# Three loads behind a scatter in a new order, and one block's transposes moved by a few matmuls

## The chip, the cores and the metric

The kernel runs on one core of one Trainium2 chip. The metric is the device time of one execution in microseconds; the figures are medians over several executions. One further execution was taken with the hardware profiler, and every duration below is from that one.

## What is computed

One layer over 4096 tokens of 256 features: a dense graph layer, then causal attention with rotary embeddings, then a mixture of 8 experts of which each token takes two.

```python
x = x + gnn(layernorm(x), adj)            # x: (4096, 256), adj: (4096, 4096)
x = x + ffn(layernorm(x))

def gnn(f, adj):
    h = adj @ (f @ neigh_W.T) / (adj.sum(axis=1, keepdims=True) + 1.0)
    return concatenate([f, h], axis=-1) @ lin_W.T

def ffn(x):                               # one sequence of 4096 tokens
    h = rmsnorm(x)
    q, k, v = ...                         # 4 heads, 2 key/value heads of 64, rotary
    y = softmax(causal(q @ k.T / 8)) @ v
    x = x + y @ wo.T
    flat = rmsnorm(x)
    probs = softmax(flat @ router_w.T)
    ...                                   # the two largest of 8, made to sum to one
    out = sum over e of weight[:, e] * ((silu(flat @ w1[e].T) * (flat @ w3[e].T)) @ w2[e].T)
    return x + out
```

All data are float32. The experts have 682 hidden features.

## The kernel before

The order of the instructions on each engine is the order in which the program writes them (`tc.manual_schedule()`, L94). Semaphore waits between engines follow from the tiles that are read and written. SyncE (SP) issues nearly all loads, GpSimd (POOL) the scatters. An instruction that waits holds back everything behind it on its own engine.

**The graph layer (L253 to L682).** Tokens lie in eight blocks of 512. `adj` comes as 64 blocks of 512 x 512 (1 MB each) through three buffers (`load(n)`, L268). `aggregate(b, steps)` (L510) makes the products of one row of eight adjacency blocks with the normalised features `g[jb]`. Each block's 2 x 2 product of sub-blocks is made with seven products instead of eight, from sums that VectorE (DVE) makes: `halve(n)` (L478) the sums S1 to S4 of an adjacency block, `halve_x(b)` (L455) the sums T1 to T4 of the features. The first products of a block (A11, A12) take the adjacency block as it was loaded. After the fourth product (`i == 3`, L538) `aggregate` calls the list `steps[jb]`, and after the seventh `steps[jb, "end"]`. The preparation of later feature blocks stands in these lists:

- `scales_x(b)` (L437): mean and variance on VectorE, the inverse deviation on GpSimd
- `normed_x(b, t)` (L443): VectorE writes the normalised block into `g[b]`. It is called from `features(b - 1)`
- `turned_x(b)` (L450): eight transposes on TensorE (L431) into two banks, two copies by ScalarE (L433)
- `features(b)` (L494): `normed_x` of the block after it, then eight matmuls in the program (L503, sixteen in the trace), added to the residual by VectorE (L508)

Blocks 0, 1 and 2 are turned before `aggregate` starts, in the startup sequence L635 to L658; blocks 3 to 7 in the `"end"` lists.

**Attention (from L686)** goes over the blocks in a fixed order and keeps TensorE in matmuls of scores and values. At its end it also routes tokens: rows of normalised tokens, with their gates, are scattered in device memory (`lists`) by expert.

**The expert groups (L1875 to L1923).** The rows of each expert are cut into groups: 25 whole groups of 256 rows and, of 128 rows, up to 21 half groups. The loop runs over the first 42 of them (`NM`) in the order `TURNS`. For group `k`:

- `load_rows(k)` (L1393) loads the rows, 265 KB or half of it. The room is a ring of five; that of group k + 4 held group k - 1, whose scatter takes its row numbers from it. So this load waits until the scatter of group k - 1 has landed
- `load13(k)` (L1379) loads w1 and w3 of the group's expert (1408 KB), `load2(k)` (L1386) loads w2 (768 KB), both into rings of five. `load13` and `load_rows` first read their expert or place from a table
- `prepare(k)` (L1407) turns the rows on TensorE, during the group before
- `hidden(k)` (L1672) or, for 13 of the whole groups, `hidden_seven(k)` (L1486) makes the hidden features. The second form needs sums of w1 and w3, which GpSimd makes some groups ahead: `sums13` (L1451, L1463 to L1466)
- `combine(k)` (L1726) makes the products with w2, the gates are applied (L1765 or L1771), and GpSimd scatters each half with an added sum into `acc_dram` (L1776). A scatter waits until the group's before has landed

In iteration k, after `combine(k - 1)`, GpSimd writes a one-element tile and SyncE copies it out (`sent`, L1910 and L1911). As GpSimd takes instructions in order, SyncE passes this marker only once the scatter of group k - 1 has been issued. Then SyncE issues the loads for later groups: rows of k + 4, w2 of k + 4, w13 of k + 5. At k = 39 the accumulated rows are copied to the output (L1922); the last three groups are scattered into the output itself.

```python
            if 0 < k < NM - 1:
                combine(k - 1)
                if k + 4 < NM:
                    nc.gpsimd.memset(sent, 0.0)
                    nc.sync.dma_start(sent_dram, sent)
            if k + 4 < NM:
                load_rows(k + 4)
                load2(k + 4)
            if k + 5 < NM:
                load13(k + 5)
```

Of the kernel before, what the change touches and what calls it, by code (L numbers as in the profile page):

```python
# [54 lines left out]
NM = NG - RARE  # L55
# [11 lines left out]
def fast_kernel(  # L67
# [185 lines left out]
    with (  # L253
# [171 lines left out]
        def transposed(src, dst):  # L425

            for h in range(2):
                tr = p_tr.tile([P, 2, 2, P], F32, tag="tr", name="tr")
                for t in range(2):
                    for c in range(2):  # L430
                        nc.tensor.transpose(tr[:, c, t, :], src(2 * h + t, c), ident)  # L431
                cols = slice(h * 2 * P, (h + 1) * 2 * P)
                nc.scalar.copy(dst[:, :, cols], tr.rearrange("p c t i -> p c (t i)"))  # L433
# [16 lines left out]
        def turned_x(b):  # L450

            turned[b] = qT[b % 4]
            transposed(lambda t, c: g[b][:, t // 2 * 2 + c, t % 2, :], turned[b])

        def halve_x(b):  # L455

            nc.scalar.copy(
                g[b][:, 1:4:2, :, HC - 1], ones[:, 0:4].rearrange("p (k t) -> p k t", k=2)
            )
            part = [g[b][:, k] for k in range(7)]  # L460
            nc.vector.tensor_sub(part[T1], part[G12], part[G11])
            nc.vector.tensor_sub(part[T3], part[G22], part[G12])
            nc.vector.tensor_sub(part[T2], part[G22], part[T1])
            nc.vector.tensor_sub(part[T4], part[T2], part[G21])
# [29 lines left out]
        def features(b):  # L494
            fT = turned.pop(b)
            for t in range(TB if b + 1 < NB else 0):
                normed_x(b + 1, t)
            for h in range(2):
                pj = p_pj.tile([P, 2, C], F32, tag="pj", name=f"pf_{b}_{h}")
                for t in range(2):  # L500
                    for c in range(2):
                        at = (2 * h + t) * P
                        nc.tensor.matmul(  # L503
                            pj[:, t, :], fT[:, c, at : at + P], l1_sb[:, c, :],
                            start=(c == 0), stop=(c == 1),
                        )
                x1 = res[b][:, 2 * h : 2 * h + 2, :]
                nc.vector.tensor_add(x1, x1, pj)  # L508
# [144 lines left out]
        scales_x(2)  # L653
        halve(0)
        features(1)
        turned_x(2)
        halve_x(1)
        scales_x(3)  # L658
        steps = {jb: [] for jb in range(NB)}
        for jb in range(NB):  # L660
            for f, b in (
                (halve, jb + 1), (features, jb + 2), (halve_x, jb + 2), (scales_x, jb + 4),
            ):
                if b < NB or f is halve:
                    steps[jb].append(lambda f=f, b=b: f(b))
            if jb + 3 < NB:
                steps[jb, "end"] = [lambda b=jb + 3: turned_x(b)]
        steps[3].append(load_rest)
        for jb, f in ((5, scale_rest), (6, bounds), (6, turn_wo), (7, router_wo)):
            steps[jb].append(f)  # L670
        behind, at_end = [], []
        for b in range(NB):
            if b:

                steps = {0: behind, (0, "end"): at_end}
# [10 lines left out]
    with (  # L686
# [360 lines left out]
        def free(inst, group, reason):  # L1047
            tc.declare_no_dep(inst.ins, group=group, reason=reason)

        def join(inst, group):  # L1050
            tc.add_to_no_dep_group(group, inst.ins)
# [288 lines left out]
        def entry(t, most):  # L1340
            return nc.values_load(
                t, engines=[SP], min_val=0, max_val=most,
                skip_runtime_bounds_check_because="the lists are as long as the tokens are many",
            )
# [31 lines left out]
        def halves(i):  # L1376
            return HALF if i < NW else 1

        def load13(k):  # L1379
            i = TURNS[k]  # L1380
            expert_of[i] = entry(table[0:1, 1, i : i + 1], NE - 1)
            nc.sync.dma_start(
                w13s[k % 5], w13[bass.ds(expert_of[i], 1)].rearrange("o p c w -> p (o c) w")
            )

        def load2(k):  # L1386
            i = TURNS[k]
            nc.sync.dma_start(
                w2s[k % 5],
                w2[bass.ds(expert_of.pop(i), 1)].rearrange("o p k c -> p (o k) c"),  # L1390
            )

        def load_rows(k):  # L1393
            i = TURNS[k]
            n = halves(i)
            at = entry(table[0:1, 0, i : i + 1], NE * REG - (GR if i < NW else 0))
            r = late[:, LATE_ROWS + k % 5 * 2 * ROW : LATE_ROWS + (k % 5 + 1) * 2 * ROW]
            r = r.rearrange("p (h c) -> p h c", h=HALF)
            get = nc.sync.dma_start(
                r[:, 0:n, :], lists[bass.ds(at, n * P), :].rearrange("(h p) c -> p h c", p=P)  # L1400
            )
            if i < NA:
                free(get, "late writes", "the rows of the first groups are whole by then")
                join(get, "first reads")
            rows[i] = r
# [45 lines left out]
        def sums13(k):  # L1451

            if not unsummed or unsummed[0] > k + 5 or len(sums13_of) == 2:
                return
            k = unsummed.pop(0)
            chunks = w13s[k % 5][:, :, 0 : 2 * NF * P].rearrange(
                "p c (k r i) -> p c r k i", r=2, i=P
            )
            m = {f"A{r + 1}{c + 1}": chunks[:, c, r] for r in range(2) for c in range(2)}
            for n, name in enumerate(("S1", "S2", "S4")):  # L1460
                m[name] = rooms13[SPLIT13.index(k) % 2][:, n]
            m["S3"] = m["A21"]
            nc.gpsimd.tensor_add(m["S1"], m["A21"], m["A22"])  # L1463
            nc.gpsimd.tensor_sub(m["S2"], m["S1"], m["A11"])
            nc.gpsimd.tensor_sub(m["S4"], m["A12"], m["S2"])
            nc.gpsimd.tensor_sub(m["S3"], m["A11"], m["A21"])  # L1466
            sums13_of[k] = m
# [151 lines left out]
        def sums2(k):  # L1619

            if k in parts_of:
                return
            m = {}
            for c in range(2):
                weights = w2s[k % 5].rearrange("p (j c) o -> p c j o", c=2)[:, c]
                for h in range(2):
                    m[f"G{c + 1}{h + 1}"] = weights[:, :, h * P : (h + 1) * P]
            for n, s in enumerate(("T1", "T2", "T4")):
                m[s] = vv[SEVEN.index(k) % 2 * 3 + n][:, 0:3, :]
            m["T3"] = m["G12"]  # L1630
            nc.vector.tensor_sub(m["T1"], m["G12"], m["G11"])
            nc.vector.tensor_sub(m["T3"], m["G22"], m["G12"])
            nc.vector.tensor_sub(m["T2"], m["G22"], m["T1"])
            nc.vector.tensor_sub(m["T4"], m["T2"], m["G21"])
            parts_of[k] = m
# [242 lines left out]
        def step():  # L1878
            for f in next(rest, []):
                f()  # L1880
# [8 lines left out]
        for k in range(NM):  # L1889
            if k == 3:  # L1890
                sc_scope.close()
                p_h.append(ctx_h.enter_context(tc.tile_pool(name="e_h", bufs=6, space=PSUM)))
            if k == NM - 1:


                between = iter([lambda: None, lambda: combine(k - 1)])
            if k in SPLIT13:
                hidden_seven(k, step, k + 1)
            else:
                hidden(  # L1900
                    k, step if k < NM - 1 else lambda: next(between)(),
                    k + 1 if k + 1 < NM else None,
                )
            step()
            if k + 1 in SPLIT13 and TURNS[k] >= NW:
                sums2(k + 1)
# [3 lines that stand above are left out]
                    nc.gpsimd.memset(sent, 0.0)  # L1910
                    nc.sync.dma_start(sent_dram, sent)  # L1911
            if k + 4 < NM:
                load_rows(k + 4)
                load2(k + 4)
            if k + 5 < NM:
                load13(k + 5)
            if 0 < k < NM - 1:
                step()
                if k >= ALONE and TURNS[k - 1] < NW:
                    sums13(k)  # L1920
            if k == NM - LAST:
                nc.sync.dma_start(out, acc_dram[0:N, :])  # L1922
# [741 lines left out]
```

## Time and profile before

| | us |
|---|---|
| median of three runs | 1541.14 |
| lowest and highest run | 1536.98, 1544.27 |
| the profiled execution, as timed | 1537.88 |
| its span, first to last instruction | 1535.9 |
| graph layer, roughly | 0 to 500 |
| attention and routing, roughly | 500 to 1020 |
| expert groups, roughly | 1030 to 1527 |
| last scatters landing | to 1535.9 |

The profile speaks of the engines as PE (matmuls), PEld (loading of weights into TensorE), DVE, ACT (ScalarE), POOL and SP. A line of a group gives line, engine, operation, the tile written and the tiles read. In a timeline line, the first two numbers are start and duration in us, and the bracket at the end says how long the engine had stood idle and what released it. A line of waits gives total, number and longest. A line of stretches gives its length, then for each engine the busy time and the instructions in brackets, and at the end the granted clock of TensorE, the busy share of the DMA engines and GB/s. "SPq" lines are DMA issues of SyncE. Queue q1 carries the loads of SyncE, q0 the scatters of GpSimd.

### The profile page before, as it was taken

The numbers are of one execution on the slowest core, as the hardware profiler recorded it, in microseconds if no ns is written. First come the engines' busy times: TensorE is split into PE (matmuls) and PEld (weight loads), VectorE is DVE, ScalarE is ACT, GpSimd is POOL, SyncE is SP. The second block draws the span as 40 slices with busy tenths as digits, with TensorE's granted clock in tenths as the row PEclk, the third lists the DMA queues.
The fourth block names the chain that finished last, engine by engine and source line by source line (L and its number), as shares of the span: only waits on it lengthen the run. The fifth ranks groups of instructions, "written<-read, shape, count | busy, mean of one in ns | idle before, by whom it ended". The sixth has DMA issues, their size and how long they took to land. (4 is left out here: it accounts for less than half of the span.)

```text
span 1535.9 us, 28140 instructions
## 1 busy us (share of the span) xinstructions
PE 1519.8 (99%) x10925; PEld 1123.7 (73%) x10925; DVE 1056.2 (69%) x2182; ACT 555.7 (36%) x989; POOL 557.6 (36%) x641
## 2 busy tenths in 40 slices
PE   8999999999999999999999999999999999999997
PEld 7888888888888544444444444358899999999996
DVE  7754665755755677779879878884665777675862
ACT  2102021021021455655665655652123334333331
POOL 2102122121221331374554653442424446354542
PEclk9999999999999999999999999999999999999999
DMA  6334544544544000010011011047766777777765
GB/s 240 125 123 149 174 141 144 157 149 136 178 139 153 5 1 24 21 58 30 30 58 37 29 37 36 22 185 281 215 211 196 241 255 229 255 247 231 265 186 133
DMA packets 69594, 212.15 MB, mean 138 GB/s; under 512 B 17898, under 2 KB 45930, under 8 KB 55818
## 3 DMA queue, kind: packets, MB, share of 16 engines
q1 hardware_dynamic: 55914, 191.99, 36.3%
q0 software_dynamic: 12720, 17.47, 5.9%
q8 instruction: 88, 1.44, 0.4%
q10 hardware_dynamic: 816, 0.79, 0.2%
q14 instruction: 56, 0.46, 0.1%
HBM read 184.48 MB, written 27.13 MB: 138 GB/s over the span
## 5 line engine op out<-in xcount | busy, mean ns | idle before, releaser
L782 PE MATMUL sc<-qT_all,kT 64*64 64x512 f32 (+3 forms) x2304 | 282.1, 557 | 0.5 <-ACT pt_all L790 0.3
L532 PE MATMUL acc<-a,g 128*128 128x256 f32 x1024 | 244.0, 379 | 0.0
L532 PEld LDWEIGHTS acc<-a,g 128*128 128x128 f32 x1024 | 193.4, 190 | 31.7 <-issue 6.7
L782 PEld LDWEIGHTS sc<-qT_all,kT 64*64 64x64 f32 x2304 | 91.2, 133 | 128.6 <-issue 109.2
L790 ACT ACTIVATE pt_all<-sc 128x1024 f32<-128x1024 f32 (+3 forms) x157 | 148.8, 954 | 96.6 <-PE sc L782 94.6
L532 PE MATMUL acc<-more_sums,g 128*128 128x256 f32 x512 | 126.2, 379 | 0.0
L810 DVE TENSOR_TENSOR late<-late,pt_all 128x1024 f32<-128x1024 f32 (+3 forms) x91 | 107.5, 1182 | 24.3 <-POOL pt_all L792 9.8
L1776 POOL DMA_INDIRECT acc_dram<-y,late x40 | 62.7, 1568 | 163.2 <-ACT y L1765 75.3
L433 ACT COPY qT_all<-tr 128x512 f32<-128x512 f32 x30 | 16.3, 589 | 261.2 <-PE tr L431 261.0
L532 PEld LDWEIGHTS acc<-more_sums,g 128*128 128x128 f32 x512 | 97.2, 190 | 13.2
L824 PE MATMUL y_first<-pt_all,vv 64*64 64x512 f32 (+3 forms) x448 | 106.6, 554 | 0.0
L625 POOL TENSOR_TENSOR rot<-rot,tables 128x512 f32<-128x512 f32 x21 | 33.9, 1614 | 198.7 <-ACT rot L621 158.4
L1698 PE MATMUL h<-late,qT_all 128*128 128x256 f32 (+1 forms) x616 | 105.2, 327 | 0.0
L824 PE MATMUL y_second<-pt_all,vv 64*64 64x512 f32 (+3 forms) x436 | 104.2, 555 | 0.0
L1698 PEld LDWEIGHTS h<-late,qT_all 128*128 128x128 f32 x616 | 94.0, 191 | 9.6 <-ACT late L1419 0.8
L1060 POOL DMA_INDIRECT lists<-row,slots x64 | 87.5, 1367 | 17.1 <-issue 14.3
L1705 DVE TENSOR_TENSOR late<-si,h 128x256 f32<-128x256 f32 (+2 forms) x87 | 39.9, 467 | 74.1 <-ACT si L1704 43.1
L1704 ACT ACTIVATE si<-h 128x256 f32<-128x256 f32 (+2 forms) x87 | 36.5, 421 | 147.2 <-PE h L1698 138.0
L824 PE MATMUL y_third<-pt_all,vv 64*64 64x512 f32 (+3 forms) x372 | 88.7, 555 | 0.0
L621 ACT ACTIVATE rot<-pq 32x512 f32<-32x512 f32 x84 | 49.5, 589 | 82.6 <-DVE qT_all L619 43.6
L810 DVE TENSOR_TENSOR sum_all<-sum_all,pt_all 128x1024 f32<-128x1024 f32 (+3 forms) x51 | 56.0, 1097 | 15.5 <-POOL pt_all L792 9.2
L790 ACT ACTIVATE late<-sc 128x1024 f32<-128x1024 f32 (+3 forms) x55 | 50.9, 927 | 41.4 <-PE sc L782 38.5
(490 smaller groups left out, 3349.6 us busy)
## 6 DMA issues: line engine op xcount, KB each, us to landing
a<-in_adj_dram SPq DMA_DIRECT2D x64, 1024.0 KB
qT_all<-in_w_dram SPq DMA_DIRECT2D x18, 1408.0 KB
pt_all<-in_w_dram SPq DMA_DIRECT2D x16, 1408.0 KB
res_all<-in_w_dram SPq DMA_DIRECT2D x17, 768.0 KB
pt_all<-in_w_dram SPq DMA_DIRECT2D x16, 768.0 KB
res_all<-in_w_dram SPq DMA_DIRECT2D x8, 1408.0 KB
qT_all<-in_w_dram SPq DMA_DIRECT2D x9, 768.0 KB
late<-lists SPq DMA_DIRECT2D x25, 265.0 KB
```

The costliest lines, as they stand in the source:

```text
L532: nc.tensor.matmul(acc[bank][:, at, :], g[jb][:, right, k, :], m[left][:, k, :], start=(jb == 0 and k == 0 and at == 0), stop=(jb == NB - ...
L621: nc.scalar.activation(rot[n * Q : (n + 1) * Q, :], pj[(n ^ 1) * Q : ((n ^ 1) + 1) * Q, :], AF.Copy, scale=1.0 if n % 2 else -1.0,)
L625: nc.gpsimd.tensor_mul(rot, rot, tables[b][:, 1, :])
L782: nc.tensor.matmul(ps[k * HP : (k + 1) * HP, j, :w], kT[sb][hd, i * P + k * HP : i * P + (k + 1) * HP], qT[b][hd, p, off:], start=True, st ...
L790: nc.scalar.activation(pt[:, :, :w], ps[:, :, :w], AF.Exp, scale=HD ** -0.5)
L810: nc.vector.tensor_add(sums[b, p][:, :, off:], before[:, :, off:], pt[:, :, : 512 - off])
L824: nc.tensor.matmul(accs[b, p][k][hd, off:], vv[sb][some, i, hd], pt[some, j, : 512 - off], start=(s == order_of(b)[0]), stop=(s == order_o ...
L1060: put = nc.gpsimd.indirect_dma_start(out=lists[:, :], out_offset=bass.IndirectOffsetOnAxis(ap=chosen[b][:, k, t, :], axis=0), in_=flats[b] ...
L1698: nc.tensor.matmul(ps[m % 2][:, m // 2 - q, :], w13_sb[:, c, m * P : (m + 1) * P], xT[:, c, :], start=(c == 0), stop=(c == 1),)
L1704: nc.scalar.activation(si[:, 0:both, :], ps[0][:, 0:both, :], AF.Silu)
L1705: nc.vector.tensor_mul(hT[:, q : q + both, :], si[:, 0:both, :], ps[1][:, 0:both, :])
L1776: put = nc.gpsimd.indirect_dma_start(out=(acc_dram if k < NM - LAST else out)[:, :], out_offset=at, in_=y[:, h, :], in_offset=None, comput ...
```

## The change

There are two parts.

In the startup sequence `turned_x(2)` no longer stands between `features(1)` and `halve_x(1)`. It goes into the list `steps[0]`, as its second entry, so that it runs in the first call of `aggregate` after the fourth of the seven products of the first adjacency block, behind `halve(1)` and ahead of `features(2)`. VectorE's instructions keep their order, as `turned_x` has none there. On TensorE its eight transposes move behind four products (eight matmuls in the program). On ScalarE its two copies move behind the one small copy of `halve_x(1)`.

In the loop over the groups the three loads of an iteration are issued in the order w2, w13, rows instead of rows, w2, w13. The marker ahead of them stays where it was, and each load keeps the waits that its own buffers need.

```diff
@@ -653,7 +653,6 @@
         scales_x(2)
         halve(0)
         features(1)
-        turned_x(2)
         halve_x(1)
         scales_x(3)
         steps = {jb: [] for jb in range(NB)}
@@ -665,6 +664,7 @@
                     steps[jb].append(lambda f=f, b=b: f(b))
             if jb + 3 < NB:
                 steps[jb, "end"] = [lambda b=jb + 3: turned_x(b)]
+        steps[0].insert(1, lambda: turned_x(2))
         steps[3].append(load_rest)
@@ -1910,10 +1910,11 @@
                     nc.gpsimd.memset(sent, 0.0)
                     nc.sync.dma_start(sent_dram, sent)
             if k + 4 < NM:
-                load_rows(k + 4)
                 load2(k + 4)
             if k + 5 < NM:
                 load13(k + 5)
+            if k + 4 < NM:
+                load_rows(k + 4)
             if 0 < k < NM - 1:
                 step()
```

## The prediction

> **What bounds the kernel now.** I read the profiled execution in this order: busy shares, the waits of TensorE, busy time by stretch, then the two places that the change touches.
>
> ```profile
> span 1535.9 us, 28140 instructions
> PE 1519.8 (99%) x10925; PEld 1123.7 (73%) x10925; DVE 1056.2 (69%) x2182; ACT 555.7 (36%) x989; POOL 557.6 (36%) x641
> ...
> PE tr L431 <- DVE g L445: 2.8, 2, 2.2
> PE hA L1525 <- ACT qT_all L1531: 0.9, 1, 0.9
> PE ye_y L1655 <- DVE late L1615: 0.8, 1, 0.8
> ...
> 1040.00:1400.00 360.00, 360.00 (x2578) 341.35 (x2577) 235.02 (x607) 121.24 (x296) 157.51 (x187) 1.00 0.74 234
> 1440.00:1480.00 40.00, 38.30 (x311) 37.12 (x310) 32.98 (x68) 14.40 (x37) 23.36 (x24) 1.00 0.81 260
> 1520.00:1536.00 16.00, 7.16 (x34) 5.96 (x32) 1.81 (x4) 0.76 (x2) 6.06 (x7) 0.86 0.31 38
> ```
>
> TensorE is the bound: it idles 16.1 us in all (1535.9 less 1519.8). By stretch that is 4.5 us before 40 us (3.56 and 0.91), 0.9 in attention, 2.05 among the expert groups (0.35 and 1.70 after 1400 us) and 8.84 in the tail, where only the last scatters land. The change adds and removes no matmul, so nothing can be gained beyond this idle time, and of it the tail is out of reach. Place one is the first long gap:
>
> ```profile
> 14.96 3.72 PE L503 MATMUL pf<-qT_all 128*128 128x256 f32 x16 [0.24 <-ACT qT_all L433]
> 20.91 1.32 PE L431 MATMUL tr<-ident,g 128*128 128x128 f32 x8 [2.23 <-DVE g L445]
> 22.06 1.89 PE L532 MATMUL acc<-a,g 128*128 128x256 f32 x8
> 25.52 0.81 PE L503 MATMUL pf<-qT_all 128*128 128x256 f32 x3
> ...
> 20.36 1.37 DVE L445 TENSOR_SCALAR g<-res_all,mv,rstd 128x256 f32<-128x256 f32 x4
> 28.80 1.38 DVE L445 TENSOR_SCALAR g<-res_all,mv,rstd 128x256 f32<-128x256 f32 x4
> ```
>
> The transposes of block 2 stand 2.23 us for the normalised block, which VectorE makes only after the sums of the first adjacency block. Place two is SyncE's queue behind a scatter:
>
> ```profile
> 1433.28 0.29 SPq L1911 DMA_DIRECT2D sent_dram<-sent  x1
> 1440.36 0.39 SPq L1399 DMA_DIRECT2D late<-lists  x1
> 1441.00 0.35 SPq L1388 DMA_DIRECT2D res_all<-in_w_dram  x1
> 1441.86 0.35 SPq L1382 DMA_DIRECT2D pt_all<-in_w_dram  x1
> ...
> 1391.08 0.61 POOL L1910 MEMSET sent<- 1x1 f32 x1
> 1397.96 1.53 POOL L1463 TENSOR_TENSOR res_all<-pt_all 128x640 f32<-128x640 f32 x1 [6.27 <-DMA pt_all<-in_w_dram]
> ```
>
> The rows' load waits until the scatter before has landed (7.1 us from 1433.28 to 1440.36), and w2 and w13, which need no such thing, stand behind it. The waits of the SyncE queue put 77.0, 38.5 and 27.8 us on this line, 143 us in 36 waits, 4.0 each. GpSimd in turn waits for w13 before it makes sums of it: 27.1 us in six waits (14.5, 10.7 and 1.9 at L1463). TensorE shows none of this.
>
> **What the Trainium skill says.** "DMA: Bandwidth & Descriptors", section "Queues, rings and completion order": each DMA engine takes turns between the queues it has work for, a packet at a time. The trace agrees only in part: scatters issued at 1440.96 and 1442.82 moved nothing on queue q0 in 1441 to 1446 us, while q1 moved 1.34 MB, and then shared. Same page, "Issuing engines are not separate DMA queues": all transfers run on the same 16 engines, so an earlier load costs whatever else is in flight. "GPSIMD Engine Reference", section 1: GpSimd shares its SBUF interfaces with VectorE, in contention with instructions that have two SBUF inputs. The trace agrees: one pick (L1427) took 2.48 us beside GpSimd's sums at 1443.5 us, against a median of 0.168. "TensorE: Matmul & The Clock Gate", "Why this matters for your kernels": idle gaps over some 3 us cost clock. The gap removed is 2.23 us and the clock in 0 to 40 us reads 1.00, so no clock is to be won.
>
> **Part one, the transposes of block 2.** They now come after four of the seven first products. These need rows A11 and A12 of the loaded block (its landing alone), then S2 (its VectorE instruction ends at 19.11) and S3 (20.43). Block 1's features end issuing at 14.96 + 3.46 = 18.42 (3.46 is the step from 22.06 to 25.52 too: 16 matmuls of 0.216). So the products start at 18.42, reach S2 after 1.73 at 20.15 and S3 at 21.0, both ready, and end at 21.88. The normalised block 2 is there at 21.73, so the transposes run at once, to 22.9. Their copy by ScalarE follows 0.64 later and takes 0.54 (32.20 against 31.56 for the next block), so features of block 2 start at about 23.15 with a stall of 0.24, as block 1 had. Before: 25.52. TensorE is 2.3 us ahead here.
>
> Not all of it stays. VectorE's order is unchanged and it has no gap from 16 to 38 us, so the next block is still normalised at 28.80 to 30.18. TensorE gets to its transposes at 23.15 + 3.46 + 2.6 (three products) = 29.2 and follows VectorE through them, ending at about 30.5 instead of 32.4. That leaves 1.9. The block after is normalised at 38.55, before TensorE's 40.1, so no more is lost. ScalarE's small copy into block 1 now stands ahead of these copies (22.74 before), which is free: its reader at 22.98 waited for VectorE's own queue. The adjacency loads follow TensorE and move with it; the DMA share is 0.37 in 20 to 40 us. Bounds: 0 if something makes the first product wait for all sums of its block until 20.43, then 0.4; at most 2.3. I take 1.9.
>
> **Part two, the order of loads.** SyncE issues the same three loads; the rows move behind w2's one and w13's one instruction (two issues and a table read, 1.5 us from 1440.36 to 1441.86). Thirty-six w2/w13 pairs go out about 4 us earlier in the mean and 7 at best, right after the marker that follows the scatter's issue. Their buffers are free by then: combine and hidden of those groups are over. Cost on TensorE: nothing, as it never waits for a load. The rows come later in the queue: their wait for the scatter stays, and ahead of them are 2.2 MB, at 260 GB/s some 8 us, part of it already drained. They are asked for at 1440.36 and transposed at 1472.32, so 32 us cover it; without that cover each late block would cost its lateness directly. Behind the rows' wait stand only the marker and the loads of the next group, which need that scatter's successor anyway. In the first round the rows move behind a w13 that waits for TensorE until 1040.95, 5 us later, with 50 us in hand.
>
> What comes earlier: w13 is there when GpSimd asks. In the case shown it was issued at 1389.10, and would go out near 1380 behind the marker at 1378.64, so the 6.27 us go. GpSimd's 27.1 us are off the path: the sums start earlier, meet other VectorE instructions, and the 2.05 us of TensorE idling among the groups, which began beside such sums, may shrink or double. I bound this at -2 and +3 and take -0.3.
>
> What gets late next: the scatter. With loads issued at the same moment it took 8.9 us to land (1442.82 to 1451.7); in the tail, undisturbed, 3.6 (1493.47 to 1497.1). Now loads follow the second half's issue by about 2.2 us (marker 1.6 us after, then w2), by when the scatter's rows should be on the engines, so I expect landings nearer 5 than 9. Being off TensorE's path, that is worth 0.
>
> **Sum.** 1537.88 - 1.9 - 0.3 = 1535.7 against the profiled execution's own time (span 1535.9 and 2.0 around it). The median of the three runs is 3.3 above it; carried over, 1541.14 - 2.2 = 1538.9. That is 0.14%; runs of this kernel differ by 0.47%, so about 0.5% is what a measurement can tell from no change.
>
> **Rivals.** (a) The start's gain is lost to VectorE and new collisions of GpSimd's sums with it cost about 2 us: 1537.9 + 3 on the median's footing, about 1541. For it: VectorE is full at the start; against: its gap-free stretch ends at 38.5 with TensorE still behind it. (b) The runs above the profiled one (1541.14, 1544.27) lost their 3 to 6 us to late DMA among the groups, and earlier loads end that: 1535.7 less the remaining stalls, about 1534. For: the profiled run shows DMA 0.74 to 0.81 busy there; against: no wait of TensorE on a DMA in it. (c) Slower: w2 and w13 ahead starve the scatter. Place: queue q0 beside q1 in 1160 to 1480 us. Beside w13 it got some 19, 28 and 31 packets in successive us from 1446; a whole group has 288, so 9.6 us after a start of 5.3, plus 0.6 to the next: 15.5; a half group 10.7; mean 13 against a marker every 10.5 us (1178.67 to 1473.84 in 28). It decides once the mean exceeds 10.5: 2.5 us of lag in each of 28 groups, 70, less the 32 us of cover, gives 38 at worst; as queues empty between loads I take 25: 1566. Against: the scatter is issued first.
>
> **Numbers.** Forecast 0.66 (1538.9, own spread 1535 to 1543), (a) 0.16, (b) 0.08, (c) 0.10. Over 0.5% faster means under 1533.4, slower means over 1548.8: (b) gives most of 0.07, (c) 0.10, the rest 0.83. The range 1532 to 1546 takes in the costs' bounds (-4.3 and +3 on the median) and the spread of runs.
>
> **What would show it.** Right: no 2.2 us gap before L431 at 21 us and features of block 2 near 23.2; w2 issued within a microsecond of the marker; GpSimd's waits for DMA at L1463 under 5 us in all; TensorE idle near 14 us. Wrong: the first product waiting for VectorE until 20.4; scatters landing 10 us or more after issue with TensorE waiting for rows or weights in the last 400 us; a tail longer than 8.8 us.

## The result, and the profile after

The changed kernel takes 1532.32 us in the median of eight executions (1532.22 to 1532.47). The kernel before, run beside it, takes 1538.85 (eight executions, 1536.10 to 1544.27). The ratio is 0.9955, with a 95% interval of 0.9942 to 0.9968. The gain is 6.5 us where 2.2 was forecast, and the spread of the executions falls from 8.2 us to 0.25.

The profiled execution takes 1532.31 us, which is 5.57 less than the one before. First its page:

```profile
span 1530.5 us, 28132 instructions
PE 1518.1 (99%) x10925; PEld 1122.9 (73%) x10925; DVE 1056.4 (69%) x2182; ACT 555.6 (36%) x989; POOL 556.8 (36%) x641
```

The work of every engine is what it was. TensorE idles 1530.5 - 1518.1 = 12.4 us, 3.7 less than before. But the span is 5.4 shorter, so 1.7 us came out of time that the profile had counted as busy: the ends of matmuls are modelled, and a short stall can lie inside such a "busy" time. The first place, TensorE at the start (timeline):

```profile
18.60 1.89 PE L532 MATMUL acc<-a,g 128*128 128x256 f32 x8
...
22.06 1.04 PE L431 MATMUL tr<-ident,g 128*128 128x128 f32 x8
23.33 3.72 PE L503 MATMUL pf<-qT_all 128*128 128x256 f32 x16 [0.24 <-ACT qT_all L433]
...
30.44 1.89 PE L532 MATMUL acc<-a,g 128*128 128x256 f32 x8
```

The first adjacency products start at 18.60 and not at 22.06. The transposes of block 2 (L431 at 22.06) find their data, features of block 2 start 2.19 us earlier, and at the second adjacency block (30.44, before 32.43) 1.99 us are left. TensorE's list of waits holds what remains:

```profile
PE tr L431 <- DVE g L445: 0.6, 1, 0.6
PE pf L503 <- ACT qT_all L433: 0.5, 2, 0.2
```

The two waits among the expert groups are gone from this list. Stretches of the groups:

```profile
1040.00:1400.00 360.00, 360.00 (x2589) 341.74 (x2588) 236.57 (x603) 121.02 (x296) 162.69 (x193) 1.00 0.78 240
1400.00:1440.00 40.00, 40.00 (x331) 39.17 (x331) 27.87 (x62) 15.54 (x38) 19.04 (x21) 1.00 0.83 251
1440.00:1480.00 40.00, 40.00 (x335) 39.28 (x334) 30.51 (x74) 15.47 (x39) 20.27 (x22) 1.00 0.71 224
```

TensorE is full in all three. Before, it was full in the first stretch too, and had 39.65 and 38.30 in the second and third: the 0.35 and 1.70 us of idling. How much this is worth is best read from the same transposes of rows (L1413) in both traces, since their position tells how far ahead TensorE is. First, middle and end in the kernel before, then in the changed one (timeline):

```profile
1027.69 0.66 PE L1413 MATMUL tx<-ident,late 128*128 128x128 f32 x4
1391.52 0.38 PE L1413 MATMUL tx<-ident,late 128*128 128x128 f32 x2
1488.37 0.60 PE L1413 MATMUL tx<-ident,late 128*128 128x128 f32 x4
...
1025.70 0.66 PE L1413 MATMUL tx<-ident,late 128*128 128x128 f32 x4
1389.32 0.38 PE L1413 MATMUL tx<-ident,late 128*128 128x128 f32 x2
1483.16 0.60 PE L1413 MATMUL tx<-ident,late 128*128 128x128 f32 x4
```

Up to 1324 us they come 1.99 earlier, all of it from the start. Then the lead grows: 2.17 at 1334, 2.20 at 1391, 2.78 at 1443, 4.98 at 1467, 5.21 at 1488. The groups gave 5.21 - 1.99 = 3.2 us, most of it between 1391 and 1467. The tail, from the end of the last matmul to the end of the span, has about its old length (1530.5 - 1521.9 = 8.6).

SyncE's queue behind one scatter now looks like this (timeline):

```profile
1437.64 0.29 SPq L1911 DMA_DIRECT2D sent_dram<-sent  x1
1438.18 0.35 SPq L1388 DMA_DIRECT2D pt_all<-in_w_dram  x1
1439.23 0.33 SPq L1382 DMA_DIRECT2D pt_all<-in_w_dram  x1
1440.12 0.33 SPq L1399 DMA_DIRECT2D late<-lists  x1
```

w2 follows the marker in 0.54 us, w13 in 1.6, and the rows 2.5 us behind the marker find the scatter landed, or nearly so. The queue's longest sum of waits on this line is now

```profile
SPq L1399 <- DMA acc_dram<-y,late: 5.7, 7, 2.2
```

where it was 77.0. A scatter lands 3.8 us after its issue in the median (7.5 at most). GpSimd no longer waits for w13 at L1463 (27.1 us before).

How that reaches TensorE is seen in the stretch with the largest loss. The kernel before, timeline of three engines:

```profile
1440.96 1.55 POOL L1776 DMA_INDIRECT acc_dram<-y,late  x1 [7.60 <-ACT hz L1531]
1443.86 2.11 POOL L1463 TENSOR_TENSOR res_all<-res_all 128x640 f32<-128x640 f32 x1
...
1443.53 2.48 DVE L1427 TENSOR_TENSOR pick<-late,mine 128x8 f32<-128x8 f32 x1
1446.12 2.02 DVE L1563 TENSOR_TENSOR late<-wqkv_sb,hy 128x512 f32<-128x512 f32 x1
1450.39 1.13 DVE L1612 TENSOR_TENSOR kT<-late 128x384 f32<-128x384 f32 x1
...
1453.35 1.38 PE L1655 MATMUL ye_y<-qT_all,late 128*128 128x128 f32 x10 [0.81 <-DVE late L1615]
```

and the changed kernel, the same instructions:

```profile
1434.17 1.55 POOL L1776 DMA_INDIRECT acc_dram<-y,late  x1 [9.00 <-ACT y L1765]
1437.05 2.13 POOL L1463 TENSOR_TENSOR res_all<-res_all 128x640 f32<-128x640 f32 x1
...
1440.75 0.16 DVE L1427 TENSOR_TENSOR pick<-late,mine 128x8 f32<-128x8 f32 x1
1441.02 1.95 DVE L1563 TENSOR_TENSOR late<-wqkv_sb,hy 128x512 f32<-128x512 f32 x1
1445.21 0.56 DVE L1612 TENSOR_TENSOR kT<-late 128x384 f32<-128x384 f32 x1
...
1449.38 1.50 PE L1655 MATMUL ye_y<-qT_all,late 128*128 128x128 f32 x12
```

Before, the scatter was issued at 1440.96, though its tile had been ready since about 1437.3: the one before it landed only at 1440.3. The bracket names ScalarE, which had long been done; it was a DMA. GpSimd's four sums, behind the scatter, so ran from 1443.86 to 1451.1, beside VectorE's chain to the features. There a pick takes 2.48 us instead of 0.16, and the first sum of L1612 twice its 0.56. TensorE then stands at L1655. After, the scatter goes out when its tile is ready, the sums run 6.8 us earlier and meet only one long VectorE instruction, and L1655 waits for nothing.

### The profile page after: what moved, and what is told of

The parts are those of the page before. It is cut to its first block, busy times and chain, and to the rows that moved or that the text cites. A ratio compares the mean times of both kernels' runs of the same rounds, so it can differ in the third digit from the quotient of the medians.

```text
span 1530.5 us, 28132 instructions
## 1 busy us (share of the span) xinstructions
PE 1518.1 (99%) x10925; PEld 1122.9 (73%) x10925; DVE 1056.4 (69%) x2182; ACT 555.6 (36%) x989; POOL 556.8 (36%) x641
## 5 line engine op out<-in xcount | busy, mean ns | idle before, releaser
L1060 POOL DMA_INDIRECT lists<-row,slots x64 | 87.4, 1366 | 17.1 <-issue 14.3
L790 ACT ACTIVATE late<-sc 128x1024 f32<-128x1024 f32 (+3 forms) x55 | 50.9, 927 | 41.4 <-PE sc L782 38.4
```

Of the source, the lines that this page charges most:

```text
L790: nc.scalar.activation(pt[:, :, :w], ps[:, :, :w], AF.Exp, scale=HD ** -0.5)
L1060: put = nc.gpsimd.indirect_dma_start(out=lists[:, :], out_offset=bass.IndirectOffsetOnAxis(ap=chosen[b][:, k, t, :], axis=0), in_=flats[b] ...
```

## The experiments

Every ratio is against the kernel before, run beside it on the same chip. That kernel's median is not the same everywhere: 1537.73 us beside runs 1 to 4, 1539.96 beside runs 5 to 8, 1541.41 beside runs 9 to 11, and 1538.85 beside the changed kernel. So times from different sets compare less well than ratios.

**1. Part one alone.** The loop over the groups as before (the order rows, w2, w13), block 2 turned among the products.

> Only the transposes of block 2 are moved; the loads keep the order rows, w2, w13. Theory L (late sums: the rows' wait holds w13 and lets loads meet the scatters, so GpSimd scatters and makes its sums of w13 late, and these then slow VectorE where TensorE waits for it): 2.0 us under before, about 1536.9, with TensorE still idle 2 us or more among the groups and runs that differ by several us. Rival P (the two parts only work together, the shift of 2 us re-phases the groups): little or no gain beyond 0.5 us, or over 4.

Measured: 1535.73 us (22 executions, 1532.88 to 1539.98), ratio 0.9985 [0.9977, 0.9994]. The waits of TensorE among the groups stay:

```profile
PE hA L1525 <- ACT qT_all L1531: 0.9, 1, 0.9
PE ye_y L1655 <- DVE late L1615: 0.5, 1, 0.5
```

and so do GpSimd's for w13 (12.2 and 10.8 us). So part one gives 0.06 to 0.23%, and a spread of 7 us remains without the gap at the start.

**2. Part two alone.**

```diff
+        turned_x(2)
         halve_x(1)
-        steps[0].insert(1, lambda: turned_x(2))
```

> Only the order w2, w13, rows; block 2 is turned where it was. Theory L: 4.5 us under before, about 1534.3, runs within 0.5 us of one another, no idle TensorE among the groups, no wait of GpSimd for w13, the 2.23 us gap at 21 us still there. Rival P: under 2 us of gain.

Measured: 1535.20 us (17 executions, 1534.26 to 1536.76), ratio 0.9982 [0.9975, 0.9989]. The first gap stays, the waits among the groups are gone, and the scatters land in

```profile
DMA to landing us min/median/max: 3.6/3.8/5.2
```

The median is 2.5 us under the kernel before, where 4.5 were expected. Part two alone gives 0.11 to 0.25%, no less than part one, where the forecast had a sixth of it. The two sum to 0.33%; runs 3 and 4, which hold both parts and ran beside the same kernel before, give 0.35 and 0.34%.

The executions were expected within 0.5 us of one another and spread over 2.5. The profiled one (1536.10) shows a reason, at the gap that stays:

```profile
21.06 1.51 PE L431 MATMUL tr<-ident,g 128*128 128x128 f32 x8 [2.23 <-DVE g L445]
22.37 3.42 PE L532 MATMUL acc<-a,g 128*128 128x256 f32 x8
...
22.00:26.00 4.00, 4.00 (x14) 3.33 (x13) 3.68 (x10) 1.13 (x4) 0.00 (x0) 0.57 0.65 205
```

Behind the gap the granted clock of TensorE is 0.57 in the mean of 22 to 26 us, and the eight products take 3.42 us. In the kernel before the same gap left the clock at 1.00, and they took 1.89. At its first transposes of rows TensorE is 3.82 us behind the changed kernel (1029.52 against 1025.70), and near the end 3.80 (1486.96 against 1483.16). So this execution lost everything at the start and nothing among the groups. In the seven executions of 1535.70 us and more the mean clock reads 0.998 or 0.997; in the other ten it reads 0.999. That fits such a drop in the seven, though the length of the tail also moves this mean.

**3. w13 last.** The order w2, rows, w13: only w13 stands behind the wait for the scatter.

```diff
                 load2(k + 4)
+                load_rows(k + 4)
             if k + 5 < NM:
                 load13(k + 5)
-            if k + 4 < NM:
-                load_rows(k + 4)
```

> Both parts, but with the order w2, rows, w13: w13 again stands behind the rows' wait for the scatter, w2 doesn't. Theory L with w13's lateness as the cause: GpSimd waits 10 us or more for w13 in all and TensorE idles again among the groups, 1534 to 1537. Theory L with the meeting of loads and scatters as the cause: scatters land within some 5 us as w2 alone follows them, w13 is early enough, and the time is within 0.5 us of the changed kernel, 1532.3.

Measured: 1532.61 us (1532.25 to 1533.37), ratio 0.9965 [0.9952, 0.9978]. The rows' wait is long again (29.8 + 13.5 + 10.6 = 54 us), yet scatters land in 3.9 in the median, GpSimd does not wait for w13 at L1463, and the interval takes in the changed kernel's ratio of 0.9955. So w13 does not need to be free of the wait, as long as w2 is.

**4. Rows first, but without the wait.** Rows of k + 3 instead of k + 4: their room's scatter has landed long ago, so that the old order holds nothing back.

```diff
+            if 0 < k and k + 3 < NM:
+                load_rows(k + 3)
             if k + 4 < NM:
                 load2(k + 4)
             if k + 5 < NM:
                 load13(k + 5)
-            if k + 4 < NM:
-                load_rows(k + 4)
```

> Both parts, but rows first again and asked for one group later (rows of k + 3 instead of k + 4), so that their room has long been free and they don't wait for the scatter just issued. Theory L: what mattered is the wait at the head of the queue and not the order, so within 0.5 us of the changed kernel, 1532.3. Rival O (the order itself matters: the rows' many small packets ahead of the weights delay them or the scatter): 1534 or more.

Measured: 1533.20 us (1532.26 to 1533.24), ratio 0.9966 [0.9953, 0.9979]; landing 3.8 in the median. The interval takes in 0.9955 as well. With run 3: what cost is a wait ahead of both weight loads, not which load goes first.

**5. The sums later, everything else as changed.** 25 memsets of 0.229 us on GpSimd, some 5.7 us, ahead of each group's sums, in the changed kernel.

```diff
+            spend()      # a helper: 25 times nc.gpsimd.memset(spare, 0.0)
             nc.gpsimd.tensor_add(m["S1"], m["A21"], m["A22"])
```

> The changed kernel with 25 memsets of a spare 128 x 128 tile on GpSimd ahead of each of the 13 sums of w13, some 3 to 6 us each time. Theory S (TensorE's idling among the groups came from sums that ran late and slowed VectorE just before TensorE needed it): TensorE idles again at several of the 13 groups, 1535 to 1545. Rival D (the idling came from DMA or scatters being late in themselves, GpSimd's sums have nothing to do with it): within 0.5 us of 1532.3.

Measured: 1541.58 us (1540.12 to 1542.77), ratio 1.0006 [0.9994, 1.0017]; by the ratios that is 0.5%, some 8 us, above the changed kernel. TensorE's waits (lines are numbered seven higher here, so that L1532 is the L1525 of the other kernels and L1662 their L1655):

```profile
PE hA L1532 <- ACT wqkv_sb L1538: 3.6, 3, 1.7
PE hA L1532 <- ACT qT_all L1538: 2.6, 3, 0.9
...
PE ye_y L1662 <- DVE vv L1640: 1.1, 1, 1.1
```

These are the places where the kernel before lost. GpSimd has much idle time, but when its sums run decides what VectorE's instructions cost. A scatter also stands behind the memsets, so part of the 8 us may be its delay; experiment 6 bears on that.

**6. The same memsets behind the sums.** Nearly the same GpSimd work, with the sums in time.

```diff
             nc.gpsimd.tensor_sub(m["S3"], m["A11"], m["A21"])
             sums13_of[k] = m
+            spend()
```

> The control: the same 25 memsets behind the sums, so that only the next scatter is held up by the same time. Theory S: within 1 us of 1532.3. Rival D (a late scatter is what costs): as much above the changed kernel as the run with the delay ahead of the sums, or more.

Measured: 1562.54 us (1562.03 to 1563.47), ratio 1.0144 [1.0124, 1.0164]. What was expected from late sums alone, within 1 us of 1532.3, fell; what the rival expected, as much as in run 5 or more, came. So run 6 is no control for run 5. Scatters still land in 3.9 us in the median, but the memsets hold up their issue, hence the marker, hence all loads, and TensorE waits for rows (14.5 us in nine waits at L1419). Late loads then make the sums late, which gives the plainest picture of the meeting (timeline; L1469 is the L1463 of the other kernels, L1619 their L1612):

```profile
1329.38 1.53 POOL L1469 TENSOR_TENSOR sum_all<-qT_all 128x640 f32<-128x640 f32 x1 [4.05 <-DMA qT_all<-in_w_dram]
...
1329.41 1.92 DVE L1619 TENSOR_TENSOR kT<-late 128x384 f32<-128x384 f32 x1
...
1336.82 1.38 PE L1662 MATMUL ye_y<-pt_all,late 128*128 128x128 f32 x10 [1.25 <-DVE late L1622]
```

VectorE's four instructions from L1619 take 1.92, 1.79, 1.78 and 1.77 us instead of 0.56, and TensorE stands for the last. It also means that runs 5 and 6 do not separate late sums from late scatters; that the meeting costs is seen in the traces, how much of the 8 us it makes is open.

**7. Without the marker.** The changed kernel without the `sent` tile and its copy: w2 and w13 no longer wait for the scatter of their round to be issued. They go out behind the rows of the round before, that is once the scatter before has landed, ahead of the next one.

```diff
-                if k + 4 < NM:
-                    nc.gpsimd.memset(sent, 0.0)
-                    nc.sync.dma_start(sent_dram, sent)
```

> The changed kernel without the marker, so that w2 and w13 go out as soon as their rooms are free, ahead of the scatter of the group before instead of behind it. If loads ahead in the queue starve a scatter: scatters take 6 us or more to land in the median instead of 3.8, some sums are late again, 1533 to 1537. If they don't: within 0.5 us of 1532.3.

Measured: 1537.80 us (1534.32 to 1539.55), ratio 0.9985 [0.9974, 0.9997]; by the ratios 0.3%, some 5 us, above the changed kernel. The scatters' landing:

```profile
DMA to landing us min/median/max: 3.6/8.5/10.4
```

and TensorE waits again:

```profile
PE ye_y L1655 <- DVE late L1615: 3.4, 2, 1.8
PE hA L1525 <- ACT wqkv_sb L1531: 1.5, 3, 0.9
```

Earlier loads are no gain in themselves. When they lead, a scatter takes 8.5 us. In the changed kernel loads start just behind a scatter and have nearly drained when the next one's packets move: for the scatter issued at 1434.17 the loads' last packets start before 1435, its own from 1436 on.

**8 and 11. Without the sums, in both orders.** S1 to S4 of w1 and w3 are not made: in their place stand one copy, which still waits for w13, and twelve memsets, so `hidden_seven` works on other numbers. Run 8 has part one and the old order, run 11 the whole change.

```diff
-            nc.gpsimd.tensor_add(m["S1"], m["A21"], m["A22"])
-            nc.gpsimd.tensor_sub(m["S2"], m["S1"], m["A11"])
-            nc.gpsimd.tensor_sub(m["S4"], m["A12"], m["S2"])
-            nc.gpsimd.tensor_sub(m["S3"], m["A11"], m["A21"])
+            nc.gpsimd.tensor_copy(m["S1"], m["A21"])
+            for s in ("S2", "S4", "S1") * 4:
+                nc.gpsimd.memset(m[s], 0.0)
```

> Part one alone with the old order of loads, and GpSimd's sums of w13 replaced by one copy (which waits for w13 as the first sum did) and twelve memsets of about the same total time: the sums S1 to S4 of w13 aren't made, so the hidden features of 13 groups aren't the reference's. Loads and scatters meet as before. Theory S: the idling among the groups goes all the same, runs within 1 us of one another, 1532 to 1533.5. Rival D: as part one alone, a median of about 1535.7 and a spread of several us.

> Both parts of the change, and in place of GpSimd's four sums of w1 and w3 one copy and twelve memsets (S1 to S4 are not made, so hidden_seven works on other numbers). Theory E (the spread of the old order is that of the late scatters at the end, not of the sums): runs within 1.5 us of each other, 1530 to 1532.5 us, where the same kernel with the old order spread over 8 us. Rival (the spread comes from elsewhere, such as the start): runs spread by 3 us or more as with the old order.

Measured: old order 1533.05 us (11 executions, 1530.18 to 1538.43), ratio 0.9953 [0.9937, 0.9968]; new order 1530.23 (four, 1529.99 to 1530.78), ratio 0.9933 [0.9916, 0.9950]. In the profiled execution with the old order TensorE no longer idles among the groups, its last run of matmuls starts at 1519.28 as against 1519.19 in the changed kernel, and yet the executions spread over 8 us. Between runs 8 and 11 the order still makes 0.20%, against 0.30% between run 1 and the changed kernel. The intervals are wide, but late sums are one route and not the only one. Another shows at the end of this run, the last scatter into `acc_dram` and the copy of the sums to the output (timeline; line numbers are one or two lower here):

```profile
1492.32 1.56 POOL L1775 DMA_INDIRECT acc_dram<-pt_all,late  x1 [3.67 <-issue]
...
1496.12 0.60 SPq L1921 DMA_DIRECT2D out_dram<-acc_dram  x1
```

and in the changed kernel:

```profile
1488.25 1.55 POOL L1776 DMA_INDIRECT acc_dram<-pt_all,late  x1 [7.50 <-ACT pt_all L1765]
...
1492.04 0.60 SPq L1923 DMA_DIRECT2D out_dram<-acc_dram  x1
```

In run 8 the scatter stands 3.67 us for the one before, which was issued at 1486.94 and landed at 1491.60, and the copy goes out 4.1 us later. The scatters of the last three groups go into the output behind this copy, one after another. From the copy's issue to the end of the span it is 38.7 us in the kernel before, 38.4 in run 1, and 38.5 in the changed kernel (1530.5 - 1492.04); it is 36.8 in run 8 and 36.9 in run 11. So what delays the copy delays the end, also when TensorE is in time. In the profiled execution of the kernel before, this route cost nothing of its own: its last scatter into `acc_dram` went out at 1493.47, 5.22 us behind that of the changed kernel, which is TensorE's 5.21. Run 11, with the copy at 1492.02, is 1.6 us shorter than the changed kernel in the span only behind it; what shortens that part without the sums stays open.

**9 and 10. The new order in one part of the loop.** Both have part one. Run 9 has the new order from k = 30 on and the old one before, run 10 the reverse.

```diff
+            if k + 4 < NM and k < 30:      # run 10: k >= 30
+                load_rows(k + 4)
             if k + 4 < NM:
                 load2(k + 4)
             if k + 5 < NM:
                 load13(k + 5)
-            if k + 4 < NM:
+            if k + 4 < NM and k >= 30:     # run 10: k < 30
                 load_rows(k + 4)
```

> Both parts of the change, but the new order of the three loads only from k = 30 on (the last eight rounds that still load rows); before that rows, w2, w13 as in the kernel before. Theory E (the gain of the order is made at the end of the groups: late scatters there meet the sums and hold the copy of the sums to the output, which opens the chain of the tail): the time is that of the changed kernel, 1531.5 to 1533.5 us, and runs lie within 1.5 us. Theory T (it is spread evenly over all the groups, a little at each collision): a quarter of the difference, so 1534.5 to 1535.5 us, with the spread of the old order.

> The mirror of the run before: both parts of the change, the new order only for k below 30 and the old one from 30 on. Theory E: about the time of part one alone, 1534.5 to 1536.5 us, with runs that differ by several us, and in the profile a scatter late near the copy to the output. Theory T: three quarters of the difference stay, 1532.5 to 1533.5 us.

Measured: run 9 1533.87 us (six executions, five of 1533.22 to 1534.28 and one of 1537.49), ratio 0.9961 [0.9946, 0.9976]; run 10 1532.42 (five, 1532.25 to 1532.90), ratio 0.9947 [0.9933, 0.9962]. The theory of the end falls, as the end in the old order costs nothing when the rounds before had the new one. An even spread does not fit well either: against 1535.73 for no round in the new order and 1532.32 for all, the last eight rounds alone give 1.9 us and the others alone 3.3, more together than the whole 3.4. (These times come from three sets, and run 1's executions alone spread over 7 us.) A third explanation came after these runs and is read from their traces. Medians from issue to landing of the scatters, by stretch:

| us | 1040 to 1180 | 1180 to 1300 | 1300 to 1400 | 1400 to 1500 |
|---|---|---|---|---|
| run 1, old order | 3.8 | 5.8 | 8.5 | 7.4 |
| run 9, new from k = 30 | 3.8 | 6.2 | 8.8 | 3.8 |
| run 10, new to k = 29 | 3.9 | 3.9 | 3.9 | 6.2 |
| changed kernel | 3.8 | 3.8 | 3.8 | 3.8 |

In the old order the lag builds up over the rounds. A late landing holds the rows' load, so w2 and w13 go out late, so they are still on the engines when the next scatter is issued, which lands late in its turn. Run 10 shows the beginning of it, where it goes over to the old order (timeline of the queue):

```profile
1396.64 0.29 SPq L1911 DMA_DIRECT2D sent_dram<-sent  x1
1399.26 0.35 SPq L1399 DMA_DIRECT2D late<-lists  x1
...
1468.96 0.29 SPq L1911 DMA_DIRECT2D sent_dram<-sent  x1
1476.03 0.40 SPq L1399 DMA_DIRECT2D late<-lists  x1
```

From marker to rows it is 2.62 us in the first old round, then in turn 2.38, 3.41, 6.39, 3.95, 5.97, 5.10 and 7.07. Run 9 goes the other way: 6.58 in the last old round, then 2.60, 7.03, 2.49 and 6.63 in the new order, and under 3 in the four rounds after (w2 and w13 alone, now ahead of the rows, make it some 2.5). By the time that run 10's lag has grown, the groups are over: GpSimd has no wait for w13 and TensorE none in the groups.

Heavier load alone does not explain this. It does have a part in the table's first step: the markers come 14.3 us apart in the mean over the first eight rounds and 10.5 after. But the last eight rounds are the same code in run 1, and there the times from marker to rows are 2.65, 6.88, 3.00, 8.12, 6.58, 7.19, 6.94 and 8.88, 50.2 us in all against 36.9 in run 10. So what a round loses depends on the rounds before it. This is seen in one trace of each run; no run varied the start of the old order by more.

## Why the prediction was wrong

**Part one was right.** The first products started at 18.60 (said: 18.42), features of block 2 at 23.33 (23.15), and 1.99 us are left where 1.9 was taken. Run 1, with 1 to 3.5 us, agrees. But it put the clock at nothing, as the gap is of 2.23 us. That held in the profiled execution of the kernel before, where the clock stayed at 1.00; in run 2's the same gap was followed by 3.41 us at half clock. So part one can also remove a loss of some 1.7 us (an estimate: half of the 3.41 us) that comes in some executions with the gap.

**Part two was right in what it does and wrong in its worth.** w2 follows the marker in 0.54 us, scatters land "nearer 5 than 9" (3.8), the rows' cover of 32 us suffices, and GpSimd's waits are gone. The steps that failed are the two that priced this. "Being off TensorE's path, that is worth 0" was said of the landing, and the -0.3 was taken from bounds of -2 and +3 for the meetings of GpSimd and VectorE. In the profiled executions the groups gave -3.2, beyond the lower bound. With the start's 1.99 and 0.2 in the tail this makes up the 5.4 us of the span. Three things were missed:

- The landing sets when the next loads and the next scatter go out, so it is on a loop, not on a branch that ends. The prediction took the 4 us of the rows' mean wait as a constant. The landing behind that wait grew from 3.8 to 8.5 us in the median (run 1).
- The bound of -2 was TensorE's idle time in the list of waits, 2.05: "nothing can be gained beyond this idle time". Another 1.2 us among the groups lay in stretches counted as busy.
- The last scatter's lateness goes straight into the copy and the tail (run 8). The tail's length was indeed "out of reach", but not its beginning. This has no part in the -3.2, and can only bear on other executions.

**The spread was a price and was not read as one.** The forecast carried the profiled execution's gain over to the median, and its median of three executions, 1541.14, was itself 2.3 above the median of eight. But the kernel before differs by 8 us from one execution to the next, the changed one by 0.25. Run 8 against run 11 and run 1 against the changed kernel show that most of this spread goes with the order of the loads, with or without sums; run 2 adds the clock at the start.

**The rivals.** (a) did not come. (b), at 1534 with a chance of 0.08, was nearest in the number. That the higher executions lost their time to late DMA fits runs 1, 8 and 11, but none of the high ones was traced. It was turned down because the profile had "no wait of TensorE on a DMA"; the DMA's lateness reached it through GpSimd and VectorE, under VectorE's and ScalarE's names. (c) did not come since the scatter is issued first, which was the argument against it; but run 7, where loads lead, shows that its starvation of the scatter is real (8.5 us), and the marker is what keeps it away.

## What to carry to other kernels

When a wait at the head of a queue holds back transfers that do not need it, ask whether their lateness delays the very event that is waited for; if so, the lag can build up over a loop, and its price is more than the stalls of one profiled round. Look at how a latency develops over the rounds, and at the spread between executions, before calling a DMA off the path. A wait of the bounding engine is named after the last engine in the chain, so follow it back until an instruction ran late or long for another reason.

## What was not expected of the hardware

- A scatter of 128 rows issued while some 2 MB of loads are under way lands in 8.5 us in the median (run 7), and in 3.8 when it is ahead of them. The Trainium skill ("DMA: Bandwidth & Descriptors", section "Queues, rings and completion order") has the engines take turns between queues packet by packet. In run 7 the scatter issued at 1432.87 moved nothing on queue q0 until 1438, while q1 moved 1.3 MB, so the trace agrees with it only from then on. Of those 5 us, 2.1 are a scatter's own: so long after the issue its first packets move in the changed kernel.
- VectorE's sums of two tiles of 128 x 384 take 0.56 us alone and 1.77 to 1.92 beside GpSimd's sums of 128 x 640 (run 6), more than three times as long; the latter take 1.53 to 1.84. Each of the four ended 0.41 or 0.42 us after one of GpSimd's had ended, as if it could not go on before.
- A gap of 2.23 us on TensorE was followed by 3.41 us at half clock in run 2 and by none in the kernel before. In run 6 a gap of 1.87 us (to 1289.13) was followed by such a drop, and one of 3.02 us (to 1464.81) was not. So the length alone does not decide. In these traces the clock changes in steps of 3.41 us: in run 2 after 17.07 us at full clock, five steps. Counted in such steps, run 2's gap (18.83 to 21.06) lies within one, from 18.63 to 22.04; in the kernel before, counted back from the clock's change at 1531.57, a step ends at 19.46 and cuts the gap into 0.78 and 1.45 us. In run 6 the 1.87 us lie within one step and the 3.02 are cut into 1.61 and 1.41; but 1.87 us of another gap there, from 1379.62 on, fell into one step without a drop. That the cut decides is thus a reading of these traces, and no run tested it.
